# Where the node order of a score row is restored: in a strided read on ScalarE, or in the transfer to DRAM

## The chip, the cores and the metric

The kernel runs on one core of one Trainium2 chip. The metric is device time in microseconds: 2461.74 us before the change, the median of three runs from 2460.16 to 2461.83. The profile is of one execution with a span of 2459.7 us.

TensorE (PE) multiplies matrices into PSUM, which has eight banks here. VectorE (DVE), ScalarE (ACT) and GpSimd (POOL) work elementwise. SyncE (SP) issues most transfers. Each engine runs its own instructions strictly in the order of the program and waits on semaphores for the others.

## What is computed

Thirty-two graphs with 512 nodes and 256 features pass through four attention layers. Each layer normalizes the features, `h = relu(layernorm(x))`, and adds the output of an attention over the graph's 512 x 512 adjacency matrix to `x`. The layers differ in how scores come about. The change concerns layers 1 and 2, where a score is the sum of one number of each node:

```python
# layer 1                                   # layer 2
e = src[:, :, None] + dst[:, None, :]       logits = s[:, :, None] + d[:, None, :]
e = jnp.where(e > 0, e, ALPHA * e)          e = exp(-leaky_relu(logits, 0.2)), 0 where adj == 0
e = jnp.where(adj > 0, e, NEG_INF)          h_prime = (e @ Hh) / rowsum(e)
h_prime = softmax(e) @ Wh                   x = x + elu(h_prime)
x = x + h_prime
```

Layer 0 has scores by a bilinear form and two rounds of `tanh(attention @ xw)`. Layer 3 has a full bilinear form plus row and column terms.

## The kernel before

**Tiles.** The 512 nodes lie in 4 tiles (NT) of 128 partitions (P). Score matrices are kept transposed: a tile `e(l, c)` has 128 source nodes of tile `c` on the partitions and all 512 target nodes along the row, so that the attention product (`attend`, L662) can take it directly as weights. Its results `bank_a` go to PSUM, two tiles at a time.

**Order.** Nothing runs in the order in which it is written. Every step is recorded as an `op` with an engine, a cost and its inputs. A cost is a pair: how long the engine is held, and when the result is there, in nanoseconds. `Plan.order` then plays these costs through, with priorities by graph and by remaining way, and with limited numbers of buffers and PSUM banks; the order in which it starts the steps is the order of the program. ScalarE's and VectorE's costs are multiplied by 1.05 there, and a transfer's result is taken to be 800 ns later than its cost says. Up to five graphs are in flight (FLIGHT), and in the middle of the run the order repeats itself graph by graph, with layer 0 of one graph beside layer 1 of the graph before it, layer 2 of the one before that, and layer 3 of another.

**The scores of layers 1 and 2** are made in `scored_values` and `leaky_exp_t`:

- L596 multiplies the features by weights with two more columns, which give both scores of a node; `scores` (L600, VectorE) copies them into `sd`, 128 x 2 x 4: partition p, which of the two, tile t. The node of `sd[p, :, t]` is t * 128 + p. `values` (L603, ScalarE) copies the rest.
- Every partition needs the whole row of 512 target scores. For the first five and last five graphs (`turned`) TensorE makes it in PSUM by transposing a broadcast (L619). For the 22 graphs between, `collect` (L624) transfers the 128 x 4 scores to DRAM, and `spread` (L628) reads this line of 2 KB back into all 128 partitions as `row`. Both are issued by SyncE.
- `collect` writes the four scores of a partition next to each other, so in DRAM, and then in `row`, the order is p * 4 + t, not the order of the nodes. `leaky` (L635, ScalarE) puts that right: it reads `row` as `"q (p t) -> q t p"`, with a step of four floats from one element to the next, adds the source's score as its bias and applies the leaky ReLU (Prelu). In the turned graphs it reads PSUM contiguously.
- `exp` (L639, ScalarE) makes the exponentials. VectorE masks them (L764 in layer 1, L791 in layer 2), and L662 multiplies.

Around that on the same engines: ScalarE also makes the exponentials of layers 0 and 3 (L700, L930), layer 3's leaky ReLU (L924), and the tanh of layer 0 (L714), which follows a reciprocal on VectorE (L711), frees the PSUM bank it reads and feeds the second round of layer 0 (L723). SyncE also issues the transposing transfers of normalized features (L483), of masks (L443) and of layer 3 (L910), and the loads of `x` (L428) and `adj` (L431).

The costs that the planner is given for the steps above are A_PRELU = (570, 693) for `leaky`, D_OUT = (550, 3500) for `collect` and D_SPREAD = (550, 4500) for `spread`.

Of the kernel before, what the change touches and what calls it, by code (L numbers as in the profile page):

```python
# [11 lines left out]
F32 = mybir.dt.float32  # L12
# [3 lines left out]
AF = mybir.ActivationFunctionType  # L16
# [3 lines left out]
P = 128  # L20
EPS = 1e-5
ALPHA = 0.2
# [10 lines left out]
def pe(n512=0, n256=0, nt=0):  # L33
    t = n512 * PE512 + n256 * PE256 + nt * PET
    return t, t + 170.0
# [4 lines left out]
A_COPY, A_HALF, A_PRELU, A_EXP, A_TANH = (477.0, 597.0), (253.0, 373.0), (570.0, 693.0), (519.0, 640.0), (373.0, 474.0)  # L40
A_BIAS, A_PRELU2 = (570.0, 687.0), (629.0, 722.0)
# [2 lines left out]
A_HALF_BIAS = (345.0, 460.0)  # L44
A_NORM, A_JOIN, V_SPLIT = (491.0, 590.0), (620.0, 767.0), (332.0, 422.0)
D_TURN = (1310.0, 2600.0)
D_OUT, D_SPREAD = (550.0, 3500.0), (550.0, 4500.0)
D_X, D_ADJ, D_ADJ0 = (550.0, 5000.0), (550.0, 12000.0), (550.0, 2500.0)
G_LOAD = (800.0, 5000.0)

# [108 lines left out]
def kernel(  # L159
# [31 lines left out]
    nc = tc.nc  # L191
    B, N, H = x.shape
    NT = N // P
# [9 lines left out]
    dram = ctx.enter_context(tc.tile_pool(name="dram", bufs=2, space=bass.MemoryType.DRAM))  # L203


    cols, pair, stat, turned = [P, HC, N], [P, NT, H], [P, NT], [P, NT, N]
# [80 lines left out]
    def load(dst, src, *keys):  # L287

        return prepare("G", G_LOAD, [], lambda: nc.gpsimd.dma_start(out=dst() if callable(dst) else dst, in_=src), *keys)

    def rows_of(w):
        return w.rearrange("(c p) k -> p c k", p=P)

    def load_column(t, v):

        return load(t, v.rearrange("(c p) -> p c", p=P))
# [5 lines left out]
    def transposed(w_sb, dst, after, *keys):  # L302
        done = []
        for c in range(HC):
            key = f"bank{next(banks)}"

            def turn(c, key):
                for r in range(HC):
                    nc.tensor.transpose(W[key][:, r * P : (r + 1) * P], w_sb()[:, r, c * P : (c + 1) * P], ident)

            def out_of(c, key):
                nc.vector.tensor_copy(dst()[:, c, :], W[key][:, : HC * P])

            a = prepare("PE", pe(nt=HC), after, partial(turn, c, key), key, *keys)
            done.append(prepare("V", V_ADD, [a], partial(out_of, c, key), key, *keys))
        return done

    def product(dst, wT, rhs, cols, after, *keys):

        done = []  # L320
        for d in range(HC):
            key = f"bank{next(banks)}"

            def multiply(d, key):
                for c in range(HC):
                    nc.tensor.matmul(W[key][:, :cols], wT()[:, c, d * P : (d + 1) * P], rhs(c),
                                     start=(c == 0), stop=(c == HC - 1))

            def out_of(d, key):
                nc.vector.tensor_copy(dst(d), W[key][:, :cols])  # L330

            cost = pe(n256=2 * HC) if cols > P else pe(nt=2 * HC)
            a = prepare("PE", cost, after, partial(multiply, d, key), key, *keys)
            done.append(prepare("V", V_ADD, [a], partial(out_of, d, key), key, *keys))
        return done

    def seven_of(w, dst, half, after, *keys):


        def blocks():  # L340
# [29 lines left out]
    a = [load(l1_sb, rows_of(l1_w), "raw0")]  # L370
# [4 lines left out]
    a = [load(l2_aug[:, :, :H], rows_of(l2_w))]  # L375
    a = ready["l2"] = a + transposed(lambda: l2_aug[:, :, :H], l2_wt, a, "raw1")
    a = a + [load_column(l2_ac, l2_a.rearrange("o n -> (o n)"))]
# [3 lines left out]
    t = transposed(l3_sb, wt3, [load(l3_sb, rows_of(l3_w), "raw2")], "raw2", "raw4")  # L381
    a = product(lambda d: awt()[:, d, :], a12_sb, lambda c: wt3()[:, c, :], H,
                t + [load(a12_sb, rows_of(l3_a12), "raw3")], "raw3", "raw4", "raw5")
    a = product(lambda d: m3_sb()[:, d, :], wt3, lambda c: awt()[:, c, :], H, a, "raw4", "raw5", "raw6")
# [4 lines left out]
    a = [load(lambda i=i: l3_wide()[:, :, i * (HALF + 1) : i * (HALF + 1) + HALF],  # L389
              rows_of(l3_w2)[:, :, i * HALF : (i + 1) * HALF], "raw8") for i in range(2)]  # L390
# [14 lines left out]
    def graph(b, adj_before, x_before):  # L405


        T = Tiles(b)

        def op(engine, cost, after, emit, *keys):  # L410
            return plan.op(engine, cost, after, emit, b, T.uses(keys))

        def two(g):
            return slice(2 * g, 2 * g + 2)
# [7 lines left out]
        def e(l, c):  # L422

            return T[f"e{l}_{c // 2}"][:, c % 2, :]
# [185 lines left out]
        def leaky_exp_t(l, ss, sign):  # L610

            turned = b < FLIGHT or b >= B - FLIGHT
            key = f"bank_r{l}" if turned else f"row{l}"
            line = []

            def turn(t):
                nc.tensor.transpose(T[key][:, t * P : (t + 1) * P],  # L619
                                    T[f"sd{l}"][:, 0, t : t + 1].to_broadcast([P, P]), ident)  # L620

            def collect():
                line.append(dram.tile([P, NT], F32, tag=f"row_{T.places['slot']['number']}", name=f"row{l}_{b}"))
                nc.sync.dma_start(out=line[0], in_=T[f"sd{l}"][:, 0, :])  # L624

            def spread():
                d = line[0]
                nc.sync.dma_start(out=T[key][:, 0, :], in_=bass.AP(tensor=d.tensor, offset=d.offset, ap=[[0, P], [1, N]]))  # L628

            def leaky(c):  # L630
                if turned:
                    row = T[key].rearrange("q (t p) -> q t p", t=NT)
                else:
                    row = T[key][:, 0, :].rearrange("q (p t) -> q t p", t=NT)
                nc.scalar.activation(e(l, c).rearrange("q (t p) -> q t p", t=NT), row, AF.Prelu,  # L635
                                     bias=T[f"sd{l}"][:, 1, c : c + 1], alpha=ALPHA)

            def exp(c):
                nc.scalar.activation(e(l, c), e(l, c), AF.Exp, scale=sign)  # L639

            a = None
            if turned:
                for t in range(NT):
                    a = op("PE", pe(nt=1), [ss[t], a], partial(turn, t), key)
            else:
                a = op("D", D_OUT, ss, collect)
                a = op("D", D_SPREAD, [a], spread, key)
            ls = [op("A", A_PRELU, [a], partial(leaky, c), key, f"e{l}_{c // 2}") for c in range(NT)]
            return [op("A", A_EXP, [x], partial(exp, c), f"e{l}_{c // 2}") for c, x in enumerate(ls)]

        def attend(l, es, vs, use):
# [23 lines left out]
        for g in range(NT // 2):  # L675
            key = f"bank_v0{g}"
# [11 lines left out]
            a = op("PE", pe(n256=8), hs[two(g)], partial(values, g, key), key, "hT0")  # L688
            vs += [op("V", V_ADD, [a], partial(biased_v, g, j, key), key, "v0") for j in range(2)]
        es = []  # L690
        for c in range(NT):
            key = f"bank_q{c}"
# [12 lines left out]
            a = op("PE", pe(n512=4), qs, partial(similar, c, key), key, "hT0", "fa0")  # L705
            a = op("A", A_COPY, [a], partial(exp0, c, key), key, f"e0_{c // 2}")
# [22 lines left out]
        a = None  # L729
        for c in range(NT):  # L730
            a = op("PE", pe(n512=4), [ys[c], a], partial(again, c), "bank_z0", "bank_z1", "y0", f"e0_{c // 2}")
        zs = [op("A", A_COPY, [a], partial(evacuate_z, k), f"bank_z{k}", "zT") for k in range(HC)]
        xs = []
        for g in range(NT // 2):
            key = f"bank_o{g}"
# [18 lines left out]
            a = op("PE", pe(n256=8), zs + ready["w1"], partial(second_conv, g, key), key, "zT")  # L754
            bs = [op("V", V_PSUM, [a] + ready["b1"], partial(biased, 2 * g + j, key), key, "z0") for j in range(2)]
            a = op("A", A_EXP, bs, partial(tanh2, g), "z0")
# [10 lines left out]
        m1 = op("V", V_HALF, [m0, hs[0]], mask1, "codeT", "mask1")  # L767
        vs, ss = scored_values(1, hs, l1_aug, ready["l1"])
        es = leaky_exp_t(1, ss, 1.0)
        es = [op("V", V_MASK, [a, m1], partial(masked1, c), "mask1", f"e1_{c // 2}") for c, a in enumerate(es)]  # L770

# [14 lines left out]
        hs = normed(2, xs)  # L786
        vs, ss = scored_values(2, hs, l2_aug, ready["l2"])
        es = leaky_exp_t(2, ss, -1.0)

        def masked2(c):  # L790
# [106 lines left out]
        ls = [(sb[c // 2, 0], sb[c // 2, 1]) for c in range(NT)]  # L897
# [35 lines left out]
        a = op("V", (334.0, 425.0), hi, highest, "crest3")  # L933
        a = op("D", D_TURN, [a], partial(turn, 0, 2), "crest3")
        a = op("V", (900.0, 1000.0), [a], tops, "crest3")
        a = op("D", D_TURN, [a], partial(turn, 1, 0), "crest3")
        row = op("A", A_PRELU2, [a], leaky_row, "crest3")
        ls = [op("A", A_PRELU2, [a, hi[c // 2]], partial(leaky3, c), f"e3_{c // 2}") for c, a in enumerate(ls)]
        ls = [op("V", V_MASK, [a, row], partial(shifted, c), "crest3", f"e3_{c // 2}") for c, a in enumerate(ls)]
# [41 lines left out]
        for g in range(NT // 2):  # L981
            u = op("V", V_MASK, us[two(g)], partial(upper3, g), "y3", "x")
            l = op("A", A_BIAS, us[two(g)], partial(exp4, g), "y3", "r3")
# [48 lines left out]
```

The softmax here doesn't subtract the row's maximum and nothing guards it: scores larger than these inputs give would overflow.

## Time and profile before

| | busy us | share of the span | instructions |
|---|---|---|---|
| PE | 2407.4 | 98% | 10700 |
| PEld (weight loads) | 1877.3 | 76% | 10700 |
| DVE | 1876.2 | 76% | 5733 |
| ACT | 1742.8 | 71% | 3233 |
| POOL | 253.8 | 10% | 315 |

| transfer | issued | count | size each | median us to landing |
|---|---|---|---|---|
| collect (L624) | SyncE | 44 | 2 KB in 128 pieces | 3.2 |
| spread (L628) | SyncE | 44 | 256 KB | 3.7 |
| planes, transposing (L483) | SyncE | 512 | | 2.4 |
| loads of adj (L431) | SyncE | 128 | 256 KB | 2.9 |

How to read the lines of the profile. A line of instructions names line, engine, operation, result <- inputs, and the shape. In the list of groups it ends with count, busy time, mean ns of one, and the engine's idle time before them with what ended it. In a timeline it begins with start and length, and idle time before it stands in brackets with its releaser. In the list of waits the three numbers are total us, times, and the longest. One matrix product of the program counts as two matmul instructions in the profile. The length of a group in a timeline includes the overlap with the next.

### The profile page before, as it was taken

Reading aid. Unit: us, or ns where it says so; the run is one execution under the profiler, and the core shown is the slowest. Engines: PE = TensorE matmul, PEld = TensorE weight load, DVE = VectorE, ACT = ScalarE, POOL = GpSimd, SP = SyncE. Lnnn points to the kernel's source line nnn. Section 1 sums busy time; section 2 is a strip of 40 time slices with the busy share of each in tenths; the row PEclk is TensorE's granted clock in tenths of the full one; section 3 lists DMA queues with packets and bytes.
Section 4 is the critical chain, followed back from the end, with each engine's and each line's share of the span. In section 5 each row is a group of like instructions: output and inputs, shape, how many; then the busy total and the mean of one; then the engine's idle time right before and its main releaser. Section 6 shows DMA issues by size and latency. Waiting matters only on the chain.

```text
span 2459.7 us, 33966 instructions
## 1 busy us (share of the span) xinstructions
PE 2407.4 (98%) x10700; PEld 1877.3 (76%) x10700; DVE 1876.2 (76%) x5733; ACT 1742.8 (71%) x3233; POOL 253.8 (10%) x315
## 2 busy tenths in 40 slices
PE   7999999999999999999999999999999999999998
PEld 4678777777777777777777777777777777777877
DVE  5468878777777877787777777777777778756888
ACT  4466777767777777777677777777776777755884
POOL 2001001110010101011101101010011011100110
PEclk9999999999999999999999999999999999999999
DMA  7223333332333322333323333233333343321221
GB/s 178 46 56 82 73 69 82 82 74 54 80 76 82 82 64 64 80 80 82 71 54 81 74 82 82 64 65 80 80 76 70 62 83 81 71 46 22 44 46 41
DMA packets 437204, 175.92 MB, mean 72 GB/s; under 512 B 393408, under 2 KB 410432, under 8 KB 437024
## 3 DMA queue, kind: packets, MB, share of 16 engines
q1 hardware_dynamic: 430976, 154.34, 29.9%
q0 software_dynamic: 5360, 18.75, 2.3%
q8 instruction: 85, 1.39, 0.2%
q14 instruction: 95, 0.78, 0.1%
q10 hardware_dynamic: 688, 0.66, 0.1%
HBM read 64.49 MB, written 16.87 MB: 33 GB/s over the span
## 4 chain that ended last, share of the span: by engine, by line
PE 73%; ACT 17%; DVE 5%; issue 3%; DMA 2%; POOL 0%; SPq 0%; POOLq 0%; ACTq 0%; DVEq 0%
PE bank_a L662 28%; PE bank_v L596 9%; PE bank_z L723 9%; ACT e L635 8%; PE bank_o L741 4%; PE bank_f L513 4%; PE bank_f L838 4%; PE bank_w L855 4%; ACT e L639 3%; PE bank_q L696 3%; PE bank_v L855 3%; PE bank_s L878 3%; ACT xn L475 2%; PE bank_v L682 2%; ACT e L700 1%
## 5 line engine op out<-in xcount | busy, mean ns | idle before, releaser
L662 PE MATMUL bank_a<-v,e 128*128 128x257 f32 (+1 forms) x4096 | 978.0, 381 | 21.8 <-ACT y L714 17.5
L662 PEld LDWEIGHTS bank_a<-v,e 128*128 128x128 f32 x4096 | 757.9, 190 | 199.9 <-issue 68.6
L488 ACT COPY hT<-planesT 128x512 uint16<-128x512 uint16 x512 | 383.2, 767 | 42.1 <-DMA planesT<-planes 41.7
L468 POOL TENSOR_TENSOR rstd<-ve,mhalf 128x2 f32<-128x2 f32 x256 | 215.2, 849 | 1891.7 <-DVE ve L465 1807.6
L475 ACT ACTIVATE xn<-x,off,rstd 128x256 f32<-128x256 f32 x512 | 277.3, 593 | 123.1 <-DVE off L471 119.3
L596 PE MATMUL bank_v<-l_aug,hT 128*128 128x258 f32 x1024 | 251.5, 383 | 3.3 <-ACT r L807 1.7
L480 DVE COPY planes<-xn 128x512 uint16<-128x512 uint16 x512 | 207.9, 422 | 43.8 <-ACT xn L475 24.1
L723 PE MATMUL bank_z<-e,y 128*128 128x512 f32 x512 | 240.6, 592 | 0.0
L696 PE MATMUL bank_q<-fa,hT 128*128 128x512 f32 x512 | 239.3, 592 | 0.0
L596 PEld LDWEIGHTS bank_v<-l_aug,hT 128*128 128x128 f32 x1024 | 192.2, 191 | 35.5 <-issue 3.6
L461 DVE BATCH_NORM_STATS2 st<-x 128x6 f32<-128x256 f32 x512 | 209.0, 408 | 6.6 <-DMA x<-in_x_dram 6.6
L635 ACT ACTIVATE e<-row,sd 128x512 f32<-128x512 f32 x176 | 207.0, 1229 | 0.0
L603 ACT COPY v<-bank_v 128x256 f32<-128x256 f32 x256 | 92.9, 375 | 90.1 <-PE bank_v L596 75.8
L639 ACT ACTIVATE e<-e 128x512 f32<-128x512 f32 x256 | 151.9, 632 | 0.0
L696 PEld LDWEIGHTS bank_q<-fa,hT 128*128 128x128 f32 x512 | 94.9, 190 | 71.4 <-issue 60.8
L723 PEld LDWEIGHTS bank_z<-e,y 128*128 128x128 f32 x512 | 96.5, 190 | 69.1 <-issue 57.9
L885 DVE SCALAR_TENSOR_TENSOR e<-bank_s,v,mask 128x256 f32<-128x256 f32 x256 | 111.1, 476 | 16.5 <-PE bank_s L878 16.3
L682 PE MATMUL bank_v<-w_sb,hT 128*128 128x256 f32 x512 | 121.4, 380 | 0.0
L703 DVE TENSOR_TENSOR e<-e,mask 128x512 f32<-128x512 f32 x128 | 87.5, 688 | 44.0 <-ACT e L700 43.9
L741 PE MATMUL bank_o<-w_sb,zT 128*128 128x256 f32 x512 | 120.4, 379 | 0.0
L513 PE MATMUL bank_f<-hT,att_sb 128*128 128x512 f32 x256 | 119.8, 593 | 0.0
L682 PEld LDWEIGHTS bank_v<-w_sb,hT 128*128 128x128 f32 x512 | 97.1, 191 | 23.9 <-issue 6.1
(134 smaller groups left out, 3702.1 us busy)
## 6 DMA issues: line engine op xcount, KB each, us to landing
adj<-in_adj_dram SPq DMA_DIRECT2D x128, 256.0 KB, 2.9
x<-in_x_dram SPq DMA_DIRECT2D x32, 512.0 KB, 5.1
out_dram<-y POOLq DMA_DIRECT2D x32, 512.0 KB, 4.1
row<-row SPq DMA_DIRECT2D x44, 256.0 KB, 3.7
planesT<-planes SPq DMA_TRANSPOSE x512, 2.4
codeT<-code SPq DMA_TRANSPOSE x128, 2.6
crest<-crest SPq DMA_TRANSPOSE x64, 2.4
raw_w<-in_L_gnn_W_dram POOLq DMA_DIRECT2D x3, 256.0 KB, 7.1
```

What stands on the lines that cost most here:

```text
L468: nc.gpsimd.tensor_tensor(T[f"rstd{l}"][:, two(g)], T[f"ve{l}"][:, two(g)], mhalf[:, two(g)], ALU.pow)
L475: nc.scalar.activation(T[f"xn{l}"][:, t, :], T["x"][:, t, :], AF.Relu, bias=T[f"off{l}"][:, t : t + 1], scale=T[f"rstd{l}"][:, t : t + 1])
L488: nc.scalar.copy(bits[:, :, :, t * P : (t + 1) * P], T[f"planesT{l}_{t}"].rearrange("p (b c) n -> p b c n", b=2))
L513: nc.tensor.matmul(T[key], w_sb[:, c, k * P : (k + 1) * P], T[f"hT{l}"][:, c, :], start=(c == 0), stop=(c == HC - 1))
L596: nc.tensor.matmul(T[key][:, :cols], T[f"hT{l}"][:, c, t * P : (t + 1) * P], w_aug[:, c, :], start=(c == 0), stop=(c == HC - 1))
L635: nc.scalar.activation(e(l, c).rearrange("q (t p) -> q t p", t=NT), row, AF.Prelu, bias=T[f"sd{l}"][:, 1, c : c + 1], alpha=ALPHA)
L639: nc.scalar.activation(e(l, c), e(l, c), AF.Exp, scale=sign)
L662: nc.tensor.matmul(T[keys[j]][:, : LEAD + H + 1 - lead], e(l, c)[:, t * P : (t + 1) * P], T[f"v{l}"][:, c, lead:], start=(c == 0), stop=(c ...
L682: nc.tensor.matmul(T[key][:, j * H : (j + 1) * H], T["hT0"][:, c, t * P : (t + 1) * P], w0_sb[:, c, :], start=(c == 0), stop=(c == HC - 1))
L696: nc.tensor.matmul(T[key], T["hT0"][:, k, c * P : (c + 1) * P], T["fa0"][:, k, :], start=(k == 0), stop=(k == HC - 1))
L723: nc.tensor.matmul(T[f"bank_z{k}"], T["y0"][:, c, k * P : (k + 1) * P], e(0, c), start=(c == 0), stop=(c == NT - 1))
L741: nc.tensor.matmul(T[key][:, j * H : (j + 1) * H], T["zT"][:, k, t * P : (t + 1) * P], w1_sb[:, k, :], start=(k == 0), stop=(k == HC - 1))
```

## The change

The order of the nodes is restored one step earlier, in `collect`: the line in DRAM is seen as `"(t p) -> p t"`, so the four scores of a partition go to four places 128 floats apart, each a piece of 4 bytes. `row` then comes back in the order of the nodes, and `leaky` reads it contiguously, in all graphs. It is meant to spare ScalarE the strided read. The planner is told of both sides: `collect` is given 5000 in place of 3500 ns until its result is there, and `leaky` outside the turned graphs A_PRELU2 = (629, 722) in place of A_PRELU. With other costs the planner makes another order, so instructions of all engines change places.

```diff
-D_OUT, D_SPREAD = (550.0, 3500.0), (550.0, 4500.0)
+D_OUT, D_SPREAD = (550.0, 5000.0), (550.0, 4500.0)
...
             def collect():
-                line.append(dram.tile([P, NT], F32, tag=f"row_{T.places['slot']['number']}", name=f"row{l}_{b}"))
-                nc.sync.dma_start(out=line[0], in_=T[f"sd{l}"][:, 0, :])
+                line.append(dram.tile([N], F32, tag=f"row_{T.places['slot']['number']}", name=f"row{l}_{b}"))
+                nc.sync.dma_start(out=line[0].rearrange("(t p) -> p t", p=P), in_=T[f"sd{l}"][:, 0, :])
...
             def leaky(c):
-                if turned:
-                    row = T[key].rearrange("q (t p) -> q t p", t=NT)
-                else:
-                    row = T[key][:, 0, :].rearrange("q (p t) -> q t p", t=NT)
-                nc.scalar.activation(e(l, c).rearrange("q (t p) -> q t p", t=NT), row, AF.Prelu,
-                                     bias=T[f"sd{l}"][:, 1, c : c + 1], alpha=ALPHA)
+                row = T[key] if turned else T[key][:, 0, :]
+                nc.scalar.activation(e(l, c), row, AF.Prelu, bias=T[f"sd{l}"][:, 1, c : c + 1], alpha=ALPHA)
...
-            ls = [op("A", A_PRELU, [a], partial(leaky, c), key, f"e{l}_{c // 2}") for c in range(NT)]
+            ls = [op("A", A_PRELU if turned else A_PRELU2, [a], partial(leaky, c), key, f"e{l}_{c // 2}") for c in range(NT)]
```

## The prediction

> **What bounds the kernel now.** I read the busy shares first, then the busy time of each engine in single stretches, then who waited for whom, and last the instructions around the one wait that matters.
>
> The page, parts 1 and 2:
>
> ```profile
> PE 2407.4 (98%) x10700; PEld 1877.3 (76%) x10700; DVE 1876.2 (76%) x5733; ACT 1742.8 (71%) x3233; POOL 253.8 (10%) x315
> PE   7999999999999999999999999999999999999998
> ```
>
> TensorE is busy in 98% of the span; only 2459.7 - 2407.4 = 52.3 us of idle time on it can be won at all. ScalarE, where the change takes work away, has 29% of slack on average, so less ScalarE work is worth only what TensorE stands waiting for it.
>
> Busy time by stretches (length, then PE, PEld, DVE, ACT, POOL, each with instruction counts, then clock, DMA share, GB/s):
>
> ```profile
> 457.30:532.60 75.30, 74.44 (x331) 58.11 (x331) 58.48 (x180) 55.66 (x102) 7.83 (x9) 1.00 0.34 74
> 984.40:1059.70 75.30, 74.44 (x331) 58.11 (x331) 58.48 (x180) 55.59 (x102) 7.83 (x9) 1.00 0.33 74
> ```
>
> In the middle the kernel repeats itself every 75.30 us, one graph per period; 74.44 us of that is TensorE work, so 0.86 us per graph is lost. The other views say to what. TensorE's waits, all of the run:
>
> ```profile
> PE bank_a L662 <- ACT y L714: 17.5, 20, 0.9
> PE bank_w L309 <- DMA raw_w<-in_L_gnn_W_dram: 11.2, 1, 11.2
> PE bank_w L326 <- DVE raw_w L312: 4.8, 2, 3.6
> ```
>
> Of the 52.3 us, 11.2 + 4.8 lie in the weight preparation at the start, 17.5 are one stall of 0.86 us repeated in 20 graphs, and most of the rest is the drain after 2040 us. The stall (timelines of TensorE, VectorE, ScalarE in one period):
>
> ```profile
> 1016.69 6.67 PE L662 MATMUL bank_a<-v,e 128*128 128x257 f32 x30
> 1024.22 1.14 PE L662 MATMUL bank_a<-v,e 128*128 128x257 f32 x4 [0.86 <-ACT y L714]
> ```
> ```profile
> 1017.36 0.69 DVE L764 TENSOR_TENSOR e<-e,mask 128x512 f32<-128x512 f32 x1 [1.25 <-ACT e L639]
> 1022.82 0.23 DVE L711 RECIPROCAL rs<-bank_a 128x1 f32<-128x1 f32 x2
> ```
> ```profile
> 1001.93 2.35 ACT L635 ACTIVATE e<-row,sd 128x512 f32<-128x512 f32 x2
> 1014.47 2.34 ACT L635 ACTIVATE e<-row,sd 128x512 f32<-128x512 f32 x2
> 1023.72 0.81 ACT L714 ACTIVATE y<-bank_a,rs 128x256 f32<-128x256 f32 x2
> ```
>
> Layer 0's first attention tile is complete on TensorE at about 1016.69 + 20 x 0.217 = 1021.0, but its reciprocal (L711) runs only at 1022.82: VectorE has been working without a gap since 1017.36, when it got layer 1's exponentials (L639) late from ScalarE. ScalarE in turn has been busy without a gap from 1001.9 to 1019.6, eight of its instructions there being L635. The tanh L714 follows the reciprocal, frees a PSUM bank, and L662 of layer 1 goes on. The chain of waits puts 8% on L635; that is the length of the burst on the path, not what TensorE loses by it (17.5 us).
>
> **What the skill says.** (1) *ScalarE: Activation LUTs*, "What ACT_TABLE_LOAD costs": an ACTIVATE with a pointer bias takes about 280 + 0.833 N ns, 707 ns at N = 512, and neighbours overlap by 93. The trace agrees for contiguous rows in SBUF (L924, same function and shape: 716 ns) and not for L635:
>
> ```profile
> L635 ACT ACTIVATE e<-row,sd 128x512 f32<-128x512 f32 x176 | 207.0, 1229 | 0.0
> L924 ACT ACTIVATE e<-e,zero 128x512 f32<-128x512 f32 x128 | 85.3, 716 | 30.9 <-DVE crest L902 30.8
> ```
>
> (2) *SBUF — State Buffer*, "Door 1", note on cachelines: lines have 16 bytes, and each access that crosses to a new one pays. L635 reads with a step of 4 floats, 16 bytes, so every element is on a new line; 1229 against 716 fits. (3) *DMA: Bandwidth & Descriptors*, "Rules for kernel authors": a non-contiguous last dimension becomes one descriptor per element. No transfer in this trace writes 4-byte pieces to DRAM.
>
> **The change part by part.** *Leaky ReLU, contiguous.* Back-to-back, L635 has a pitch of 2.35 - 1.23 = 1.12 us, L924 one of 1.34 - 0.72 = 0.62. Saved: 0.50 us x 176 = 88 us of ScalarE, 4.0 us in each of the 22 middle graphs. All lies beside TensorE work but for the stall. In the old order, 4 us off the burst would let the last L764 follow its inputs instead of ScalarE; L711 could run at 1021.2 in place of 1022.82, 1.6 us earlier, more than the 0.86 of the stall. The planner, too, was given 570 x 1.05 = 600 ns for what took 1120; with 629 x 1.05 = 660 it is now above the expected 620.
>
> *The collecting transfer.* 128 pieces of 16 bytes become 512 of 4: with the work spread over 16 engines, 32 each in place of 8. It landed in 3.2 us (median, 1.4 to 5.4). Lower bound for 24 more pieces per engine: the mean of queue q1, 16 x 2459.7 x 0.299 / 430976 = 27 ns a packet, so +0.65 us. Upper bound: the load of an attention vector in 512 pieces of 4 bytes (l_ac, 2.0 KB) took 7.3 us, from GpSimd's queue and with the engines 98% busy. I take 4.5 us and keep 3.9 and 7.3.
>
> *What waits for it.* The spread (L628) waits on SyncE for the collection, and everything behind it on that queue waits too: two transposes of layer 0's planes, one of the next mask, a load of adj. Already now 20 spreads stood 58.3 us in all. In the changed order the spread of layer 2 stands behind layer 1's collection. I laid the TensorE rows of one period of the changed order end to end with the trace's pitches (0.86 us per 512 columns, 0.43 per 256, 0.22 per 128; 75.8 - 1.7 = 74.1 us): layer 2's last scores end at 13.4, so its collection goes out at about 14.6; layer 1's last end at 22.5, its collection goes out at 23.5, layer 2's spread at 24. The first may thus take 9 us free. That spread lands 3.7 us later (median now), at 28; its eight ScalarE instructions of 0.62 and 0.52 us end by 32.5; the first layer-2 product needs the first of them at 35.0. Layer 1's spread, behind three transposes of 1.25 us, goes out at 28.2, which gives its collection 4.7 us; it lands at 32; its products come at 48, but the tanh of layer 0 stands among its exponentials: tile complete at 35.0, reciprocal behind VectorE's burst at about 36.7, tanh done by 37.2, needed by L723 at 39.4. So 2.1 us of slack, and the collection may take 4.7 + 2.1 = 6.8 us before TensorE notices.
>
> *Moved order.* The new costs make the planner rearrange the middle: TensorE's rows differ from row 378 on, and the last 414 are the same, so the drain (about 17 us of idle) and the opening (16) stay. TensorE work is the same 10700 instructions. Cost zero there: no engine's other work changes.
>
> *Sum.* 20 x 0.86 = 17.2 us go; new small stalls in graphs 5 to 10, where the new order takes longer to settle, I put at 0 to 2. 2461.7 - 17.2 + 0.5 = 2445.
>
> **Rivals.**
> (A) Forecast, stall gone: 2445. For: one cause, ScalarE's late exponentials, and the slips it came from are removed; TensorE's rows fit. Against: slack of 2 us is small, and my layout ignores bank waits.
> (B) The stall changes place: another tile waits for a bank or for a tanh, about as long. 0.4 to 1.1 us in 20 graphs: 2452 to 2467, say 2459. For: eight banks are all in use in the attention part, and the order is new. Against: every planned cost on ScalarE is now at or above the trace's.
> (C) Slower: the 4-byte pieces land late, 9 us. Then layer 1's spread, and ScalarE's queue behind it, come 9 - 6.8 = 2.2 us too late for L723, in 22 graphs: +48, less the 17 won: 2493. For: no such write is in the trace, and SyncE's queue blocks in order. Against: the first row of the bound above, and 16 engines busy to a third only.
> (D) ScalarE becomes worth its full 88 us: 2374. Against: TensorE's 2407 us of work don't allow it. No weight.
>
> **How the numbers follow.** A 0.77, B 0.13, C 0.10. The floor with the present opening and drain is 2461.7 - 17.5 = 2444; a better settling of graphs 5 to 10 and of the passage to the drain (5 us of idle in 2040 to 2390) can give a few us more, so the range begins at 2438. Above, it takes in A with some new stalls and most of B: 2461. Faster by over 0.2% means under 2456.8: A nearly whole and a third of B, 0.81. Same: the rest of A and most of B, 0.09. Slower: C with a little of B, 0.10.
>
> **What would show it.** Right: the contiguous Prelu at about 0.71 us; a period of about 74.5 us; the row of TensorE waiting for L714's tanh gone or under 3 us; TensorE busy still near 2407; the collection's landing under 6.8 us. Wrong: a new row of some 20 TensorE waits (B), or SyncE standing at the spread for over 3 us a graph with ScalarE idle before the Prelu (C).

## The result

The changed kernel takes 2711.15 us (median, 2708.17 to 2723.63) against 2461.78 us before: 1.102 times as long, interval 1.0989 to 1.1051. The forecast was 2445, with 2438 to 2461 as its range.

The profile after, parts 1 and 2 of the page:

```profile
PE 2497.4 (92%) x10700; PEld 1927.3 (71%) x10700; DVE 1870.3 (69%) x5733; ACT 1660.8 (61%) x3233; POOL 253.8 (9%) x315
...
PE   7999999899998889888998899888988889999998
```

ScalarE has lost 1742.8 - 1660.8 = 82 us of work, as intended. TensorE now idles 2721.9 - 2497.4 = 224.5 us in place of 52.3, and its busy time has grown by 90 us with the same 10700 instructions. Together that is the whole difference of the two spans, 172.2 + 90.0 = 262.2 us. In the middle a graph now mostly takes 85 to 90 us in place of 75.3 (layer 0 begins at 1066.65, for example, and again at 1156.48), and there is no longer one fixed stall but several, of changing length. Who TensorE waited for:

```profile
PE bank_s L874 <- DVE e L881: 77.7, 18, 8.4
PE bank_a L658 <- DVE e L787: 45.6, 15, 7.0
PE bank_v L596 <- ACT hT L488: 31.9, 10, 9.0
```

The old wait, for the tanh (now L710), is not among them. VectorE and ScalarE were themselves waiting, for transfers. First two of VectorE's waits, then ScalarE's groups, which show the expected Prelu and who is late:

```profile
DVE planes L480 <- DMA planesT<-planes: 183.1, 41, 9.9
DVE mask L451 <- DMA codeT<-code: 84.5, 16, 7.8
```

```profile
L488 ACT COPY hT<-planesT 128x512 uint16<-128x512 uint16 x512 | 381.2, 767 | 375.9 <-DMA planesT<-planes 375.3
...
L632 ACT ACTIVATE e<-row,sd 128x512 f32<-128x512 f32 x176 | 118.2, 709 | 2.8 <-DMA row<-row 2.8
```

Prelu takes 709 ns as forecast and hardly ever waits for its row, 2.8 us in the whole run. It comes to them late itself: what ScalarE waits for is the transposed features at L488, 375.3 us. The same line, and the landing of the masks, in the kernel before:

```profile
L488 ACT COPY hT<-planesT 128x512 uint16<-128x512 uint16 x512 | 383.2, 767 | 42.1 <-DMA planesT<-planes 41.7
...
codeT<-code SPq DMA_TRANSPOSE x128, 2.6
```

The transfers after, median from issue to landing:

```profile
codeT<-code SPq DMA_TRANSPOSE x128, 5.9
...
row<-sd SPq DMA_DIRECT2D x44, 2.0 KB, 10.7
```

The collection lands in 10.7 us (before 3.2), and transfers issued after it land late too: the masks (codeT) in 5.9 us in place of 2.6. The median of a whole group hides most of it. SyncE issued 192 transfers while a collection was under way, and none of them landed before it. The 86 transposes of features among them took 9.7 us (median), the other 426 took 2.4; the 22 loads of adj took 12.3 us in place of 2.9. One period, SyncE's queue and then ScalarE and VectorE:

```profile
1085.83 0.58 SPq L624 DMA_DIRECT2D row<-sd  x1
1086.50 0.45 SPq L431 DMA_DIRECT2D adj<-in_adj_dram  x1
1087.01 1.31 SPq L443 DMA_TRANSPOSE codeT<-code  x1
1088.41 2.53 SPq L483 DMA_TRANSPOSE planesT<-planes  x2
1090.99 7.26 SPq L443 DMA_TRANSPOSE codeT<-code  x1
1098.34 0.53 SPq L624 DMA_DIRECT2D row<-sd  x1
```
```profile
1099.43 1.39 ACT L488 COPY hT<-planesT 128x512 uint16<-128x512 uint16 x2 [8.42 <-DMA planesT<-planes]
1100.69 0.58 ACT L696 ACTIVATE e<-bank_q 128x512 f32<-128x512 f32 x1
1110.89 1.38 ACT L488 COPY hT<-planesT 128x512 uint16<-128x512 uint16 x2 [9.62 <-DMA planesT<-planes]
```
```profile
1099.50 0.43 DVE L480 COPY planes<-xn 128x512 uint16<-128x512 uint16 x1 [8.30 <-DMA planesT<-planes]
...
1111.33 0.69 DVE L451 TENSOR_SCALAR mask<-codeT 128x2048 bf16<-128x2048 bf16 x1 [7.75 <-DMA codeT<-code]
1111.94 0.87 DVE L881 SCALAR_TENSOR_TENSOR e<-bank_s,v,mask 128x256 f32<-128x256 f32 x2
1114.01 0.69 DVE L787 SCALAR_TENSOR_TENSOR e<-codeT,e 128x512 f32<-128x512 bf16 x1 [1.21 <-ACT e L635]
```

A collection goes out at 1085.83 and lands at 1098.4. The two transposes issued from 1088.41 on land only at 1099.4 and 1099.9, one issue (1090.99) even hangs for 7.26 us where others take 1.2 to 1.3, and ScalarE stands for 8.42 us at L488. The second collection follows at 1098.34, and it happens again. In the meantime the DMA engines move little, and then much at once (columns: length, PE, PEld, DVE, ACT, POOL, clock, DMA share, GB/s):

```profile
1088.00:1098.00 10.00, 9.95 (x43) 7.32 (x41) 2.81 (x8) 1.79 (x4) 0.00 (x0) 1.00 0.63 36
1098.00:1100.00 2.00, 0.00 (x0) 0.00 (x0) 0.50 (x2) 0.57 (x1) 0.00 (x0) 1.00 1.20 199
```

In ScalarE's program L488 stands ahead of exponentials. In VectorE's, L480 and the mask (L451) stand ahead of the evacuation of PSUM (L881) and of the masking of layer 2 (L787). TensorE then stops:

```profile
1102.84 2.07 PE L874 MATMUL bank_s<-hs,fa 128*128 128x256 f32 x4 [1.39 <-DVE e L881]
...
1114.85 6.17 PE L658 MATMUL bank_a<-v,e 128*128 128x257 f32 x16 [6.64 <-DVE e L787]
```

The last line also shows where most of the 90 us of added busy time come from: after 6.64 us of standing still, 16 matmul instructions take 6.17 us in place of 16 x 0.217 + 0.17 = 3.6. The busy times by stretches give the clock:

```profile
1115.00:1117.00 2.00, 2.00 (x5) 1.63 (x6) 2.00 (x4) 2.00 (x5) 0.00 (x0) 0.50 0.03 8
1117.00:1119.00 2.00, 2.00 (x6) 1.54 (x6) 2.00 (x6) 2.00 (x5) 0.00 (x0) 0.50 0.00 0
```

TensorE is granted half its clock after the stop. The Trainium skill (*TensorE: Matmul & The Clock Gate*, Part 1) has half rate after an idle window of about 3.4 us, until TensorE has been busy again about as long. The trace agrees in the lengths: it records 36 stretches of half clock, but for the last all of 3.41, 6.83 or 10.24 us (the kernel before has two stretches). In the idle time it differs: a stop of 2.1 us, from 1021.9 to 1024.05, was followed by half clock too. The mean granted clock fell from 0.998 to 0.958. The stretches hold 157 us of TensorE's work, which would have taken 78 us less at the full clock: so about 78 of the 90 us are the clock. What the rest is stays open.

### The profile page after: what moved, and what is told of

Its sections match the earlier page's. It is cut to its first block, busy times and chain, and to the rows that moved or that the text cites. A ratio compares the mean times of both kernels' runs of the same rounds, so it can differ in the third digit from the quotient of the medians.

```text
span 2721.9 us, 33956 instructions
## 1 busy us (share of the span) xinstructions
PE 2497.4 (92%) x10700; PEld 1927.3 (71%) x10700; DVE 1870.3 (69%) x5733; ACT 1660.8 (61%) x3233; POOL 253.8 (9%) x315
## 3 DMA queue, kind: packets, MB, share of 16 engines
q1 hardware_dynamic: 447872, 154.34, 37.7%
## 4 chain that ended last, share of the span: by engine, by line
PE 68%; DMA 19%; ACT 6%; issue 3%; DVE 3%; SPq 1%; POOL 0%; POOLq 0%; DVEq 0%; ACTq 0%
PE bank_a L658 29%; DMA planesT<-planes 17%; PE bank_z L719 8%; PE bank_v L596 6%; PE bank_q L692 4%; PE bank_o L737 4%; PE bank_f L513 4%; PE bank_w L851 3%; PE bank_s L874 3%; PE bank_v L678 2%; PE bank_f L834 2%; ACT hT L488 2%; PE bank_v L851 2%; DMA codeT<-code 1%; ACT xn L475 1%
## 5 line engine op out<-in xcount | busy, mean ns | idle before, releaser
L658 PE MATMUL bank_a<-v,e 128*128 128x257 f32 (+1 forms) x4096 | 1011.8, 389 | 63.2 <-DVE e L787 45.6
L658 PEld LDWEIGHTS bank_a<-v,e 128*128 128x128 f32 x4096 | 778.1, 195 | 251.7 <-issue 116.5
L488 ACT COPY hT<-planesT 128x512 uint16<-128x512 uint16 x512 | 381.2, 767 | 375.9 <-DMA planesT<-planes 375.3
L480 DVE COPY planes<-xn 128x512 uint16<-128x512 uint16 x512 | 213.6, 422 | 225.4 <-DMA planesT<-planes 183.1
L596 PE MATMUL bank_v<-l_aug,hT 128*128 128x258 f32 x1024 | 270.0, 391 | 35.3 <-ACT hT L488 31.9
L596 PEld LDWEIGHTS bank_v<-l_aug,hT 128*128 128x128 f32 x1024 | 194.5, 195 | 90.5 <-ACT hT L488 43.2
L692 PE MATMUL bank_q<-fa,hT 128*128 128x512 f32 x512 | 247.6, 610 | 0.0
L874 PE MATMUL bank_s<-hs,fs 128*128 128x256 f32 x384 | 111.1, 417 | 60.6 <-DVE e L881 60.6
L696 ACT ACTIVATE e<-bank_q 128x512 f32<-128x512 f32 x128 | 75.7, 595 | 116.1 <-PE bank_q L692 115.2
L874 PEld LDWEIGHTS bank_s<-hs,fs 128*128 128x128 f32 x384 | 77.2, 209 | 79.6 <-DVE e L881 64.2
L881 DVE SCALAR_TENSOR_TENSOR e<-bank_s,v,mask 128x256 f32<-128x256 f32 x256 | 111.4, 476 | 28.1 <-PE bank_s L874 27.9
```

Of the source, the lines that this page charges most:

```text
L480: nc.vector.tensor_copy(T[f"planes{l}_{t}"], bits)
L488: nc.scalar.copy(bits[:, :, :, t * P : (t + 1) * P], T[f"planesT{l}_{t}"].rearrange("p (b c) n -> p b c n", b=2))
L596: nc.tensor.matmul(T[key][:, :cols], T[f"hT{l}"][:, c, t * P : (t + 1) * P], w_aug[:, c, :], start=(c == 0), stop=(c == HC - 1))
L658: nc.tensor.matmul(T[keys[j]][:, : LEAD + H + 1 - lead], e(l, c)[:, t * P : (t + 1) * P], T[f"v{l}"][:, c, lead:], start=(c == 0), stop=(c ...
L692: nc.tensor.matmul(T[key], T["hT0"][:, k, c * P : (c + 1) * P], T["fa0"][:, k, :], start=(k == 0), stop=(k == HC - 1))
L874: nc.tensor.matmul(p[:, j * N // 2 : (j + 1) * N // 2], left(x)[:, j * P : (j + 1) * P], right(x), start=fresh and j == 0, stop=True, skip ...
```

## The experiments

Times are medians of the runs of one batch, ratios are to the kernel before on the same chip. The first question was which part of the change does it.

**The old order with both edits.** Only the planner's costs are put back.

```diff
-D_OUT, D_SPREAD = (550.0, 5000.0), (550.0, 4500.0)
+D_OUT, D_SPREAD = (550.0, 3500.0), (550.0, 4500.0)
...
-op("A", A_PRELU if turned else A_PRELU2, [a], partial(leaky, c), ...)
+op("A", A_PRELU, [a], partial(leaky, c), ...)
```

> The changed program with the planner's old costs (collect 3500 ns, leaky A_PRELU everywhere), so every engine has the order of the kernel before; only the 4-byte pieces and the contiguous read are changed. Theory Q (queue: the pieces hold the transfer queue for some 7 us, and every transfer behind them, transposes first, lands that much later): as slow as the changed kernel or nearly, 2600 to 2800 us. Theory R (row: only the row itself comes late, and ScalarE's in-order queue with it): slow too, 2550 to 2800. Theory O (order: the rearranged program is what is slow): about 2445.

Measured: 2638.74 us, 1.0708 (1.069 to 1.0725). The collection lands in 10.5 us. Theory O falls as the main cause: the old order with the 4-byte pieces is slow as well. In this order the row is waited for too. SyncE stands 324.9 us at the spreads (98.9 in the changed kernel, 58.3 before), and ScalarE waits 116.8 us for rows (2.8 in the changed kernel), beside 174.7 us at L488. So this run doesn't tell Q from R.

**The new order alone.** The kernel before, with the new costs.

> The kernel before with the planner's new costs only, so the order of the changed kernel with 16-byte pieces and the strided read. Q and R: 2450 to 2475 us, no transfer held up. O: about 2700.

Measured: 2488.92 us, 1.0106 (1.0091 to 1.0121), 14 us above what Q and R expected. TensorE waits 28.8 us in 18 places at L723 for the tanh L714: it is the place for which the forecast had worked out 2.1 us of slack, with quick Prelus ahead of the tanh; here they are slow.

**The read alone, in the old order.** `leaky` as in the change, `collect` as before; this kernel leaves out restoring the order of the nodes.

> The kernel before, in its own order, with the contiguous read alone: collection in 16-byte pieces, and the restoring of the node order left out, so the scores of layers 1 and 2 belong to permuted nodes. If the ScalarE half of the forecast was right: Prelu 0.71 us, the wait of TensorE for the tanh gone, 2445 us. If the stall in each period had another cause: 2460.

Measured: 2439.47 us, 0.9907 (0.9892 to 0.9921). TensorE's wait for the tanh is gone. ScalarE's half of the forecast holds.

**The pieces alone, waited for by nobody.**

```diff
                 nc.sync.dma_start(out=T[key][:, 0, :], in_=bass.AP(...))   # spread
+                extra = dram.tile([N], F32, tag=..., name=...)
+                nc.sync.dma_start(out=extra.rearrange("(t p) -> p t", p=P), in_=T[f"sd{l}"][:, 0, :])
```

> The kernel before with one more transfer after each spread: the same 128 x 4 scores once more to DRAM, in 512 pieces of 4 bytes, read by nobody. The row of scores itself is made as before. Q: the transposes behind it are held up all the same, 2600 to 2750 us. R: nobody waits for it, so 2460 to 2475.

Measured: 2669.32 us, 1.084 (1.0824 to 1.0857). This decides between Q and R. Nobody reads the extra line. The row's own two transfers come somewhat later (medians of 4.6 and 4.2 us in place of 3.2 and 3.7), but ScalarE waits only 12.8 us in all for rows. Yet the kernel loses 207 us, and ScalarE stands 228.1 us at L488. What costs is what the pieces do to other transfers. Their landing and that of the masks:

```profile
codeT<-code SPq DMA_TRANSPOSE x128, 7.5
...
extra<-sd SPq DMA_DIRECT2D x44, 2.0 KB, 10.5
```

**Another queue for the idle pieces** (`nc.gpsimd` in place of `nc.sync`).

> As the run with the idle pieces (one more collection per layer in 512 pieces of 4 bytes, read by nobody), but issued from GpSimd's queue instead of SyncE's. Theory Q (the pieces hold up what stands behind them in SyncE's own queue): the transposes are free again, 2460 to 2480 us. Theory D (the pieces hold the sixteen DMA engines, whatever the queue): 2600 to 2700.

Measured: 2598.57 us, 1.0557 (1.0541 to 1.0573). The extra line takes 11.9 us. SyncE's masks still land in 7.5 us and its spreads in 9.0 (medians of the 79 of 128 and the 30 of 44 whose landing this trace gives). So Q is wrong in its place: it isn't only the queue of the pieces that is held, transfers of another queue are too. D comes nearest, at the lower edge of its range; the kernel loses 137 us in place of 207.

**The same bytes in 128 pieces of 16** (`"(p t) -> p t"` for the idle line).

> As the run with the idle pieces, on SyncE's queue, but in 128 pieces of 16 bytes. Theory N (the cost goes by the number of pieces, some 7 us for 512): a quarter, about 1.8 us of hold per transfer, mostly hidden: 2465 to 2510 us. Theory F (one more transfer on this queue is what costs): 2600 or more.

Measured: 2468.61 us, 1.0027 (1.0015 to 1.0038); the extra line lands in 3.4 us. It fits N, and F falls.

**The changed program with a free collection.** New order, contiguous read, 16-byte pieces; again without restoring the order of the nodes.

> The changed program in its own order, with the collection in 16-byte pieces and the contiguous read; the restoring of the node order is left out, so the scores of layers 1 and 2 belong to permuted nodes. It is what the forecast took the changed kernel to be, with a transfer that costs nothing. If the 26 us that the new order cost with the strided read came from late Prelus: about 2440 us. If the new order has waits of its own: 2450 to 2465.

Measured: 2446.24 us, 0.9937 (0.9922 to 0.9952). This is the kernel that was forecast at 2445. Against 2439.47 in the old order, the new order costs 7 us.

**Sorting the row once on ScalarE.** A version that keeps the 16-byte collection and the old order:

```diff
             def leaky(c):
...
+                if not turned and c == 0:
+                    nc.scalar.copy(T[key][:, 1, :].rearrange("q (t p) -> q t p", t=NT),
+                                   T[key][:, 0, :].rearrange("q (p t) -> q t p", t=NT))
+                row = T[key] if turned else T[key][:, 1, :]
+                nc.scalar.activation(e(l, c), row, AF.Prelu, bias=T[f"sd{l}"][:, 1, c : c + 1], alpha=ALPHA)
```

> The kernel before in its own order, with the strided read done once: ahead of the first Prelu of a layer ScalarE copies the row into node order (into the unused half of its tile), and the four Prelus read that copy contiguously. ScalarE: 1.12 + 4 x 0.62 = 3.6 us in place of 4.5 per layer, 1.8 us less per graph. The stall of 0.86 us per graph should shrink or go: 2445 to 2455 us. If only the whole 4 us removes it: 2460.

Measured: 2437.85 us, 0.9902 (0.9887 to 0.9916), less than either kernel, and 7 us below the range expected. Sparing ScalarE some 1.8 us a graph did as much as sparing it 4 (2439.47). The 44 copies take 1133 ns each, the Prelus 712 ns; TensorE is busy in 99% of the span.

**What it is about the pieces.** Three idle lines with other shapes: 4-byte pieces 512 bytes apart; 512 pieces of 24 bytes (six floats for each node); half of the 4-byte pieces.

```diff
+extra = dram.tile([N, P], F32, ...)     # 512 bytes apart
+nc.sync.dma_start(out=extra.rearrange("(t p) s -> p t s", p=P)[:, :, 0], in_=T[f"sd{l}"][:, 0, :])
...
+extra = dram.tile([N, 6], F32, ...)     # 24 bytes
+nc.sync.dma_start(out=extra.rearrange("(t p) s -> p t s", p=P), in_=T[f"st{l}"])
...
+nc.sync.dma_start(out=extra[: N // 2].rearrange("(t p) -> p t", p=P), in_=T[f"sd{l}"][:, 0, : NT // 2])   # half
```

> The idle pieces on SyncE's queue again, 512 of 4 bytes, but each to a block of 512 bytes of its own in DRAM instead of side by side. Theory N (each piece costs some 0.2 us of an engine, wherever it goes): 2640 to 2700 us, landing about 10.5 us. Theory B (pieces that share a small block of DRAM hold each other up): well under 2550, landing 3 to 5 us.

> The idle transfer with 512 pieces of 24 bytes (other data, six floats for each node), written side by side. N (cost by the number of pieces): as with 4 bytes, 2640 to 2700 us, landing 10 to 11 us. Theory S (pieces of 4 bytes are what is slow): under 2550.

> The idle transfer with 256 pieces of 4 bytes, half of the scores, 16 per engine. By number of pieces the landing is half way between the 3.4 us of 128 pieces and the 10.5 of 512, about 5.8 us, and the time between 2469 and 2669, nearer to the first because a hold of 3 us is partly hidden: 2480 to 2560 us.

Measured: 2463.81 us, 1.0001 (0.9992 to 1.0009), for the pieces far apart; 2465.6 us, 1.001 (1.0003 to 1.0016), for 24 bytes; 2645.18 us, 1.0731 (1.0713 to 1.0748), for the half. N falls three times over: as many pieces of 4 bytes cost nothing when they lie apart, as many pieces of 24 bytes cost nearly nothing, and half as many side by side cost nearly all (they land in 9.8 us, where 5.8 was expected). S falls as well, by the pieces far apart. The same views as for the idle pieces side by side, now with 512 bytes between them:

```profile
codeT<-code SPq DMA_TRANSPOSE x128, 2.5
...
extra<-sd SPq DMA_DIRECT2D x44, 2.0 KB, 3.5
```

**How near is too near?** The same idle pieces with steps of 8, 16 and 32 bytes (`dram.tile([N, 2])`, `[N, 4]`, `[N, 8]`, first column).

> The idle transfer of 512 pieces of 4 bytes, each 8 bytes after the last in DRAM (side by side it landed in 10.5 us and the kernel took 2669; 512 bytes apart 3.5 us and 2464). Theory L (each further piece within the same small stretch of DRAM waits for the one before): half as many per stretch, landing about 7 us, time about 2550. Theory X (only pieces that touch each other are slow): 3.5 to 4.5 us, 2465.

> As the run with steps of 8 bytes, with steps of 16. L: a quarter as many per stretch, landing about 5 us, time 2470 to 2500. X: 3.5 us, 2465.

> As the run with steps of 8 bytes, with steps of 32. L: an eighth, landing about 4 us, time about 2465. X: 3.5 us, 2465. If it is still 10 us, the stretch that counts is of several hundred bytes.

| step of the 512 pieces | median landing, us | time, us | ratio |
|---|---|---|---|
| 4 bytes (side by side) | 10.5 | 2669.32 | 1.084 |
| 8 | 5.9 | 2502.24 | 1.016 |
| 16 | 4.3 | 2472.41 | 1.004 |
| 32 | 3.8 | 2465.49 | 1.0014 |
| 512 | 3.5 | 2463.81 | 1.0001 |

The 24-byte pieces touch one another and still land in 4.5 us, near the steps of 16 and 32 bytes: touching alone is not what is slow. The fall is gradual, so X falls, and L holds in its direction; but it is steeper than a share of the pieces: over the 3.5 us of pieces far apart the excess is 7.0, 2.4, 0.8 and 0.3 us, about a third at each doubling.

**The planner told the truth.** The changed kernel with `D_OUT = (7000.0, 10500.0)`: the queue is held for 7 us, the result is there after 10.5.

> The changed kernel with the planner told that a collection holds the transfer queue for 7000 ns and is there after 10500, so that the order allows for it. If the loss comes from an order that doesn't know of the hold: 2445 to 2500 us. If two holds of some 7 us per graph can't be placed without TensorE waiting: 2550 or more.

Measured: 2456.03 us, 0.9973 (0.9961 to 0.9985). The collections still take 9.3 us and the masks 5.1, as far as this trace gives their landing (5 of 44 and 13 of 128). As many transposes of features go out within 9.3 us of a collection as in the changed kernel (86 and 85), and ScalarE still waits 143.7 us for them. But in this order TensorE hardly waits for ScalarE there (5.3 us at L596 for L488, 31.9 in the changed kernel), and it is busy in 98% again. The 4-byte collection can be lived with, given an order that knows of it; it gains a quarter of a per cent then, where the single copy on ScalarE gains one.

## Why the prediction was wrong

**Step that failed first: the collecting transfer.** The forecast said "I take 4.5 us and keep 3.9 and 7.3" for its landing; it was 10.7, above its upper bound. The number of pieces was right: queue q1 carries 16896 more packets, 384 for each collection. Their price was not. The lower bound priced a piece like the mean packet of the queue, 27 ns. The upper bound was the load of 512 pieces of 4 bytes, which reads small pieces from DRAM and writes them to SBUF; this transfer writes small pieces side by side into DRAM, and the runs show that this is what costs. The trace of before held nothing like it, as the forecast said, and a bound from the opposite direction was no bound.

**Step that failed and cost the time: what waits for it.** The forecast asked only who waits for the collection to land: the spread, what stands behind the spread on SyncE, and the Prelus that read the row. By that account it could take 6.8 us before TensorE noticed. At 10.7 us the waits of that account stayed small in the changed order: SyncE stood 98.9 us at the spreads (58.3 before), and the Prelus waited 2.8 us, though they come late themselves. The forecast left out that a transfer under way can hold other transfers that are already issued: the transposed features, for which ScalarE waited 375.3 us in place of 41.7. The idle pieces, read by nobody, cost 207 us, where the same bytes in pieces of 16 cost 7. Rival C had the direction and a landing of 9 us, but priced it by the wrong wait and arrived at 2493. Of its two signs, SyncE standing over 3 us a graph at the spread came (98.9 / 22 = 4.5); ScalarE idle before the Prelu did not.

**The leaky ReLU: right.** 709 ns against 0.71 forecast, the stall for the tanh gone, and 2439.47 us by itself.

**Moved order: a small error.** "Cost zero" was 7 us with a quick collection (2446.24 against 2439.47) and 72 us with the slow one (2711 against 2639): the two orders pay by different waits. In the new one, 86 transposes of features go out while a collection is under way and are held by it; in the old one only 5 do, because SyncE stands at the spread ahead of them, and there the row itself comes late. Why the first costs more was not tried apart.

**The sum** left out that stalls of this length lower TensorE's clock; about 78 of the 262 us are that.

**Open.** What in the chip makes pieces that lie near each other slow was not settled. The Trainium skill names read-modify-write for transfers under 512 bytes (*DMA: Bandwidth & Descriptors*, "Specifications"). Size alone is not it: 4-byte pieces 512 bytes apart land in 3.5 us. Small writes to one stretch of DRAM waiting for one another would fit the ladder of steps, and is only argued. In every slow run neighbouring pieces came from neighbouring partitions; pieces side by side from one partition were not tried. How the pieces hold other transfers is open as well.

## What to carry to other kernels

Price a transfer by what it does to the transfers around it, not only by who waits for its data; a copy of it that nobody reads, added to the unchanged kernel, tells the two apart in one run. Don't scatter single floats side by side into DRAM without measuring it: here 16 bytes at a time with one sorting copy on ScalarE was cheaper. And where a planner orders the work, a wrong cost for the new transfer can be worth more than the edit itself: 2711 and 2456 us are one kernel with two numbers in one line.

## What was unexpected of the hardware

- 512 pieces of 4 bytes written to DRAM side by side land in 10.5 us, 8 bytes apart in 5.9, 32 bytes apart in 3.8, 512 bytes apart in 3.5; 512 pieces of 24 bytes side by side in 4.5, 128 of 16 bytes in 3.4.
- While they are under way, other transfers land late, those of another queue included: with the pieces issued by GpSimd, SyncE's masks land in 7.5 us in place of 2.6.
- The share of the span that packets took is a poor sign of it. Queue q1 had 37.7% in the changed kernel and 29.9% before, but 30.7% with the idle pieces side by side and 29.8% with them apart, with spans of 2666.7 and 2461.2 us. What shows it is that little is moved: in the period shown, 36 GB/s while a collection was under way and 199 right after.
- Half clock followed a stop of TensorE of only 2.1 us.
